# A graph-attention kernel: TensorE spreads the destinations' parts over the edge tiles in four parts, one in each group, instead of one burst per node tile

## The chip, the cores and the metric

The kernel runs on one core of one Trainium2 chip. The metric is device time in microseconds for one execution; 2591.09 us is the median of three runs (2585.95 to 2595.64) of the kernel before. The profile comes from a further execution, taken with the hardware profiler.

## The reference, cut to what matters

Two graph-attention (GAT) layers and a two-layer perceptron over 6250 nodes and 100000 edges that are sorted by destination, with a self-loop at each node:

```python
def gat_conv(x, src, dst, W, a_src, a_dst, bias, heads):
    h = (x @ W).reshape(n, heads, -1)
    alpha_s = (h * a_src[None]).sum(-1)
    alpha_d = (h * a_dst[None]).sum(-1)
    e = jax.nn.leaky_relu(alpha_s[src] + alpha_d[dst], NEG_SLOPE)
    m = jax.ops.segment_max(e, dst, num_segments=n)
    e = jnp.exp(e - m[dst])
    denom = jax.ops.segment_sum(e, dst, num_segments=n)
    alpha = e / (denom[dst] + 1e-16)
    out = jax.ops.segment_sum(h[src] * alpha[:, :, None], dst, num_segments=n)
    return out.reshape(n, -1) + bias
...
h = gat_conv(relu(layernorm(x)), src, dst, W1, a_src1, a_dst1, b1, 4)
h = gat_conv(relu(h), src, dst, W2, a_src2, a_dst2, b2, 1)
out = x + relu(relu(h) @ Wm1 + bm1) @ Wm2 + bm2
```

## The kernel before, in words

**Stages.** A first stage (until about 150 us of the profile) normalises x and multiplies it by W1, and stores one row for each node, features and source scores, in a table in device memory. Then `layer_edges` (L525) runs twice, for layer 1 with four heads and for layer 2 with one. While layer 1 runs over the edges it also makes layer 2's table (`Node1.steps`, L794); while layer 2 runs it also does the perceptron and writes the output (`Node2.steps`, L900). Between the two lies a short stretch (about 1430 to 1480 us) in which `prepare` (L464) and `first_whole` (L262) work.

**Tiling.** An edge tile holds 128 edges. Four edge tiles are a group `g`; four groups belong to a node tile `t` of 128 nodes, so `t, j = divmod(g, 4)` (L706). There are 49 node tiles and 196 groups in a layer. The order of the instructions is written out by hand: each engine executes its own instructions in the order of the program.

**One group.** `gather(g + AHEAD)` (L540, L709) has GpSimd issue four indirect DMAs, eight groups ahead, that fetch the rows of the edges' sources into `G`; ten such buffers exist. `pair(g, 0)` and `pair(g, 1)` (L611) treat two edge tiles each: ScalarE takes two exponentials of the source scores (L619, L621); VectorE multiplies by the destination's part `rho` (L624), takes the larger (L634 in layer 1, L627 in layer 2), and makes `hw` (L636 in layer 1: the weighted rows; L631 in layer 2: weighted one-hot matrices); TensorE sums over edges into `o_ps[g]` (L647), of which there are three buffers. `gather_up(g - 2)` (L658) comes at the end of a group: VectorE adds `o_ps` of the group two before to the running sum (`acc`, L672), ScalarE copies a quarter of it (`sum`, L680). `advance(g)` (L684) is called twice in a group and takes the node work of finished node tiles one step on: transposes (L761), `rT` (L767), `h_ps` (L812) and a table row in layer 1; `tp`/`m_ps` (L921), `mT` (L926) and `y_ps` (L937, L940) in layer 2.

**The destinations' parts.** An edge tile needs, for each of its edges, the destination's `rho`. `pre.win` holds `rho` of the nodes near each group, split into three bf16 parts. `mask[u]` is a one-hot matrix for two groups (eight edge tiles): in layer 1 VectorE makes it (`make_mask`, L559, L570) and the sync engine's queue (SP) stores it; in layer 2 SP loads it again (`fetch_mask`, L519). Six mask buffers exist. `meet(t)` (L591) multiplies the 16 mask tiles of node tile `t` with `win` into the PSUM tile `e_ps[t]`, of which there are two ("e"): 16 matmuls of 12 columns in layer 1 and of 3 columns in layer 2 (L599). `join(t)` (L602) has VectorE add the three parts for all 16 edge tiles in one instruction (L607); the sums are the `rho` that `pair` reads in the four groups of `t`.

**Order around the change.** At `j == 0` of node tile `t`, after `pair(g, 0)` and the first `advance`, `meet(t + 1)` issues all 16 matmuls (L724); `pair(g, 1)` follows. At `j == 3`, after `pair(g, 1)` and the second `advance`, comes `join(t + 1)` (L737), then `gather_up(g - 2)`. So the matmuls of `meet(t + 1)` stand three groups ahead of the VectorE instruction that reads their result.

Of the kernel before, what the change touches and what calls it, by code (L numbers as in the profile page):

```python
# [10 lines left out]
F32 = mybir.dt.float32  # L11
# [6 lines left out]
P = 128  # L18
# [11 lines left out]
TPG = 4  # L30
# [23 lines left out]
def kernel(  # L54
# [21 lines left out]
    nc = tc.nc  # L76
# [9 lines left out]
    ps = edges_stack.enter_context(tc.tile_pool(name="ps", bufs=2, space=bass.MemoryType.PSUM))  # L86
# [152 lines left out]
    def first_sources(layer):  # L239

        n = len(THERE[layer])
        sources[layer] = []
        for j in range(0, n, 8):
            m = min(n - j, 8)
            of = rowsp.tile([P, 16 * P], BF16, name="drow").bitcast(I32)
            nc.sync.dma_start(of[:, :m * P], bcast(src_rows, m * P, (FIRST + j) * P))
            sources[layer].append(of)
# [14 lines left out]
    def first_whole(pool, layer):  # L262

        j = 0
        for stage, (n, there) in enumerate(EARLY[layer]):
            if stage and layer == 1:
                first_hits(pool, layer, stage)
            for k in range(n):
                g, t = divmod(FIRST + j, TPG)
                G = first_G[layer][g][:, t]  # L270
                p = ps.tile([P, TW[layer]], F32, name="missing", tag="o", bufs=3)
                for T in range(there, NT):
                    nc.tensor.matmul(p, hits[stage, T][:, k * P:(k + 1) * P], kept[T][:, :TW[layer]],
                                     start=(T == there), stop=(T == NT - 1))
                nc.vector.scalar_tensor_tensor(G, G, first_ok[layer][:, j:j + 1], p, ALU.mult, ALU.add)
                j += 1
# [226 lines left out]
    drow, mask = {}, {}  # L503
# [9 lines left out]
    def fetch_rows(r):  # L513

        if r < NET // 16:
            drow[r] = rowsp.tile([P, 16 * P], BF16, name="drow")
            nc.sync.dma_start(drow[r], bcast(dmod_d, 16 * P, r * 16 * P))
# [7 lines left out]
    def layer_edges(layer, H, node, pre, matched, pre_pool):  # L525
# [4 lines left out]
        with tc.tile_pool(name=f"eg{layer}", bufs=4) as eg, \  # L530
# [3 lines left out]
            G, hot, e_ps, o_ps = {}, {}, {}, {}  # L534

            def tiles(g):

                return range(max(TPG * g, FIRST) - TPG * g, min(TPG * g + TPG, LAST) - TPG * g)

            def gather(g):  # L540
                if not 0 <= g < NG:
                    return
                if g in first_G[layer]:
                    G[g] = first_G[layer][g]
                else:
                    G[g] = gp.tile([P, TPG, max(TW.values())], F32, name="G")[:, :, :TW[layer]]
                for t in tiles(g):
                    k = TPG * g + t
                    if k < FIRST + len(THERE[layer]):
                        continue  # L550
                    nc.gpsimd.indirect_dma_start(  # L551
                        out=G[g][:, t], out_offset=None, in_=table[layer],
                        in_offset=bass.IndirectOffsetOnAxis(ap=src_i[:, k:k + 1], axis=0))


            def both(u):
                return tiles(2 * u)[0], TPG + tiles(2 * u + 1)[-1] + 1
# [16 lines left out]
            def make_hot(g):  # L574

                if layer == 2 or not 0 <= g < NG:
                    return
                T = tiles(g)
                k, n = TPG * g + T[0], len(T)
                hot[g] = eg.tile([P, TPG, P], F32, name="hot")  # L580
                nc.vector.tensor_tensor(  # L581
                    hot[g][:, T[0]:T[0] + n], iota_ps.unsqueeze(1).to_broadcast([P, n, P]),
                    dcol[:, k:k + n].unsqueeze(2).to_broadcast([P, n, P]), ALU.is_equal)

            def ranges(t):

                for u in (2 * t, 2 * t + 1):
                    a, b = both(u)
                    yield u, u % 2 * 8, a, b

            def meet(t):  # L591

                if t >= NT:
                    return
                e_ps[t] = ps.tile([P, 16, 6 * H], F32, name="e_ps", tag="e")
                for u, at, a, b in ranges(t):
                    m = mask.pop(u)
                    for k in range(a, b):
                        nc.tensor.matmul(e_ps[t][:, at + k, :3 * H], m[:, k * P:(k + 1) * P],  # L599
                                         pre.win[:, 2 * u + k // TPG + 1], start=True, stop=True)  # L600

            def join(t):  # L602
                if t >= NT:
                    return
                (_, _, a, _), (_, at, _, b) = ranges(t)
                T = slice(a, at + b)
                nc.vector.tensor_reduce(  # L607
                    e_ps[t][:, T, 3 * H:4 * H],
                    e_ps[t][:, T, :3 * H].rearrange("p t (h k) -> p t h k", k=3), AX.X, ALU.add)
# [40 lines left out]
            def stay_warm(n):  # L650

                if layer == 1:
                    for _ in range(n):
                        nc.tensor.matmul(idle_ps[0], idle[:, :P], idle, start=True, stop=True)
# [3 lines left out]
            def gather_up(g):  # L658

                if not 0 <= g < NG:  # L660
                    return
                last = g == NG - 1
                if last:

                    late.append(node.steps(NT - 1, None, run[0], o_ps.pop(g)))
                    return
                acc = sums.tile([P, RW[layer]], F32, name="acc")
                if g == 0:
                    nc.vector.tensor_copy(acc, o_ps.pop(g))
                else:  # L670
                    k = (g + 1) % 4
                    nc.vector.scalar_tensor_tensor(acc, run[0], keep[:, k:k + 1],  # L672
                                                   o_ps.pop(g), ALU.mult, ALU.add)
                run[0] = node.whole(NT - 1, acc) if g == NG - 2 else acc
                t, q = divmod(g - 2, 4)
                if 0 <= t < NT - 1:
                    if q == 0:
                        done[t] = sums.tile([P, RW[layer]], F32, name="sum", bufs=3)
                    r = slice(32 * q, 32 * q + 32)
                    nc.scalar.activation(done[t][r], acc[r], AF.Copy)  # L680
                    if q == 3:
                        late.append(node.steps(t, done.pop(t)))

            def advance(g):  # L684

                for _ in range(2 if NG - 4 <= g < NG - 2 else 1):
                    for step in list(late):
                        if next(step, 0) == 0:
                            late.remove(step)
# [10 lines left out]
            matched()  # L700
            if layer == 2:
                first_whole(pre_pool, layer)
            meet(0)
            join(0)
            for g in range(NG):
                t, j = divmod(g, 4)  # L706
                if g == NG - 2:
                    at_end.append(g)
                gather(g + AHEAD)  # L709
                pair(g, 0)  # L710
                if g == NG - 1:
                    pair(g, 1)
                if g >= NG - 2:
                    gather_up(g - 1)
                advance(g)
                if g <= NG - 4:
                    make_hot(g + 1)
                if g in (NG - 4, NG - 3):
                    make_hot(g + 2)
                if j == 0:  # L720
                    if layer == 1:
                        fetch_rows(t + 4)
                    node.prefetch(t)
                    meet(t + 1)  # L724
                elif j == (2 if t < NT - 1 else 1):
                    node.ahead(t)
                elif j % 2:
                    make_mask((g + 7) // 2)
                if g == NG - 3:
                    idle_ps.append(ps.tile([P, 4 * P], F32, name="idle_ps", tag="e"))  # L730
                if g >= NG - 3:
                    stay_warm(3)
                if g < NG - 1:
                    pair(g, 1)
                advance(g)
                if j == 3:
                    join(t + 1)  # L737
                if g < NG - 2:
                    gather_up(g - 2)
                if g == NG - 3:  # L740
                    gather_up(g - 1)
                if NG - 3 <= g < NG - 1:
                    stay_warm(3)
                G.pop(g)
                hot.pop(g, None)
                if layer == 1 and g == NG - 6:
                    first_sources(2)
# [505 lines left out]
```

## Time and profile before

| | us |
|---|---|
| median of three runs | 2591.09 |
| the profiled execution's own time | 2642.57 |
| its span in the profile | 2640.8 |
| layer 1 over the edges, about | 1230 (200 to 1430) |
| layer 2 over the edges, about | 1140 (1480 to 2620) |
| TensorE busy with matmuls, of the span | 1657.0 (63%) |
| GpSimd busy | 1598.5 (61%) |
| VectorE busy | 1415.1 (54%) |
| ScalarE busy | 560.3 (21%) |
| the 1564 matmuls of L599, busy | 55.7 |
| mean clock granted to TensorE | 0.764 of full speed |

The profile covers one execution from the first instruction to the last. "Busy" counts the time in which at least one instruction of the group was at work; matmuls overlap, so 1564 of them at 167 ns each are busy for 55.7 us only. An instruction's "idle before" is the time that its engine stood still ahead of it, and the arrow names what ended that: an instruction that had just finished; "issue", where nothing shown had just released it; or "remote", where a semaphore had just moved and the profile finds no instruction that ended then. In this kernel, on one core, "remote" is no other core.

### The profile page before, as it was taken

The numbers are of one execution on the slowest core, as the hardware profiler recorded it, in microseconds if no ns is written. First come the engines' busy times: TensorE is split into PE (matmuls) and PEld (weight loads), VectorE is DVE, ScalarE is ACT, GpSimd is POOL, SyncE is SP. The second block draws the span as 40 slices with busy tenths as digits, with TensorE's granted clock in tenths as the row PEclk, the third lists the DMA queues.
The fourth block names the chain that finished last, engine by engine and source line by source line (L and its number), as shares of the span: only waits on it lengthen the run. The fifth ranks groups of instructions, "written<-read, shape, count | busy, mean of one in ns | idle before, by whom it ended". The sixth has DMA issues, their size and how long they took to land. (4 is left out here: it accounts for less than half of the span.)

```text
span 2640.8 us, 26321 instructions
## 1 busy us (share of the span) xinstructions
PE 1657.0 (63%) x6763; PEld 1115.4 (42%) x6765; DVE 1415.1 (54%) x4359; ACT 560.3 (21%) x2601; POOL 1598.5 (61%) x1759
## 2 busy tenths in 40 slices
PE   9955556554655555555457366766666676676676
PEld 7843333333433333333335244444444444444454
DVE  7935556555655555555556354444445444444454
ACT  5521111111111111111112122222222222222122
POOL 7865666655665556556653666666666666666661
PEclk9977766777677677777778677787787778787878
DMA  9944445444444444444443444454444444454442
GB/s 358 339 144 145 136 126 145 124 136 122 134 138 127 133 130 138 129 129 136 130 117 105 132 128 130 146 151 146 139 140 150 146 138 142 146 151 144 131 150 75
DMA packets 157541, 383.24 MB, mean 145 GB/s; under 512 B 35543, under 2 KB 49966, under 8 KB 157382
## 3 DMA queue, kind: packets, MB, share of 16 engines
q0 software_dynamic: 75072, 209.10, 29.2%
q1 hardware_dynamic: 80940, 170.88, 19.2%
q10 hardware_dynamic: 1370, 1.48, 0.2%
q8 instruction: 58, 0.95, 0.1%
q14 instruction: 101, 0.83, 0.1%
HBM read 323.13 MB, written 58.19 MB: 144 GB/s over the span
## 5 line engine op out<-in xcount | busy, mean ns | idle before, releaser
L551 POOL DMA_INDIRECT G<-table,src_i x1545 | 1467.8, 950 | 908.1 <-issue 747.6
L647 PE MATMUL o_ps<-hw,hot 128*128 128x260 f32 x1564 | 604.3, 520 | 532.7 <-DVE hw L636 216.3
L647 PEld LDWEIGHTS o_ps<-hw,hot 128*128 128x128 f32 x1564 | 353.9, 248 | 750.2 <-DVE hw L636 301.4
L647 PE MATMUL o_ps<-G,hw 128*128 128x258 f32 x1564 | 500.2, 455 | 208.3 <-issue 107.6
L647 PEld LDWEIGHTS o_ps<-G,hw 128*128 128x128 f32 x1564 | 337.0, 227 | 342.8 <-issue 156.7
L680 ACT ACTIVATE sum<-acc 32x260 f32<-32x260 f32 (+1 forms) x384 | 159.9, 416 | 1489.1 <-DVE acc L672 829.4
L624 DVE TENSOR_TENSOR e_ps<-e,e_ps 128x8 f32<-128x8 f32 (+1 forms) x782 | 127.7, 163 | 561.5 <-ACT e L621 359.5
L672 DVE SCALAR_TENSOR_TENSOR acc<-acc,keep,o_ps 128x260 f32<-128x260 f32 (+1 forms) x388 | 185.3, 478 | 220.4 <-remote 203.7
L631 DVE TENSOR_SCALAR hw<-iota_ps,dcol,w 128x128 f32<-128x128 f32 x782 | 285.0, 406 | 31.4 <-DVE w L627 17.5
L636 DVE TENSOR_TENSOR hw<-G,e_ps 128x520 f32<-128x520 f32 x391 | 271.9, 695 | 48.3 <-DVE e_ps L634 29.8
L937 PE MATMUL y_ps<-wm,mT 128*128 128x384 f32 x392 | 197.2, 621 | 105.0 <-issue 60.6
L619 ACT ACTIVATE e<-G 128x8 f32<-128x8 f32 (+1 forms) x782 | 155.4, 199 | 95.0 <-issue 30.2
L937 PEld LDWEIGHTS y_ps<-wm,mT 128*128 128x128 f32 x392 | 82.4, 231 | 182.1 <-issue 119.8
L621 ACT ACTIVATE e<-G 128x8 f32<-128x8 f32 (+1 forms) x782 | 150.2, 192 | 0.0
L940 DVE TENSOR_TENSOR y<-y_ps,xt 128x384 f32<-128x384 f32 (+1 forms) x98 | 54.2, 553 | 175.5 <-remote 127.7
L346 PE MATMUL h_ps<-w,r 128*128 128x256 f32 x588 | 133.0, 380 | 4.3 <-ACT r L337 4.3
L581 DVE TENSOR_TENSOR hot<-iota_ps,dcol 128x512 f32<-128x512 f32 (+1 forms) x196 | 133.6, 682 | 0.0
L346 PEld LDWEIGHTS h_ps<-w,r 128*128 128x128 f32 x588 | 108.0, 190 | 21.7 <-ACT r L337 5.5
L767 ACT ACTIVATE rT<-tp,bT 128x128 f32<-128x128 f32 x196 | 60.2, 357 | 217.7 <-remote 175.8
L634 DVE TENSOR_TENSOR e_ps<-e_ps,e 128x8 f32<-128x8 f32 x391 | 68.1, 174 | 54.9 <-remote 29.8
L921 PE MATMUL tp<-rT,wm 128*128 128x128 f32 x392 | 64.9, 318 | 29.0 <-ACT rT L767 27.8
L921 PEld LDWEIGHTS tp<-rT,wm 128*128 128x128 f32 x392 | 61.9, 230 | 40.3 <-ACT rT L767 35.3
(405 smaller groups left out, 1175.0 us busy)
## 6 DMA issues: line engine op xcount, KB each, us to landing
xt<-in_x SPq DMA_DIRECT2D x96, 384.0 KB
drow<-dmod_d SPq DMA_DIRECT2D x49, 512.0 KB
mask_d<-mask SPq DMA_DIRECT2D x98, 256.0 KB
mask<-mask_d SPq DMA_DIRECT2D x98, 256.0 KB
G<-table,src_i POOLq DMA_INDIRECT x1545
xTt<-in_xT SPq DMA_DIRECT2D x49, 384.0 KB
out<-y SPq DMA_DIRECT2D x48, 384.0 KB
table<-kept SPq DMA_DIRECT2D x49, 132.0 KB
```

The source lines that it names most:

```text
L346: nc.tensor.matmul(h_ps, r[:, k], w1[:, k], start=(k == 0), stop=(k == KI - 1))
L551: nc.gpsimd.indirect_dma_start(out=G[g][:, t], out_offset=None, in_=table[layer], in_offset=bass.IndirectOffsetOnAxis(ap=src_i[:, k:k + 1] ...
L581: nc.vector.tensor_tensor(hot[g][:, T[0]:T[0] + n], iota_ps.unsqueeze(1).to_broadcast([P, n, P]), dcol[:, k:k + n].unsqueeze(2).to_broadca ...
L619: nc.scalar.activation(e1, sc, AF.Exp)
L621: nc.scalar.activation(e2, sc, AF.Exp, scale=SLOPE)
L624: nc.vector.tensor_mul(v, e2, rho)
L631: nc.vector.tensor_scalar(hw[:, t], iota_ps, dcol[:, k:k + 1], w[:, t], ALU.is_equal, ALU.mult)
L636: nc.vector.tensor_mul(hw, Gp[:, :, :RW[1]].rearrange("p t (h c) -> p t h c", h=H), w.unsqueeze(3).to_broadcast([P, 2, H, C + 1]))
L647: nc.tensor.matmul(o_ps[g], l, r[:, :RW[layer]], start=(k == tiles(g)[0]), stop=(k == TPG - 1))
L672: nc.vector.scalar_tensor_tensor(acc, run[0], keep[:, k:k + 1], o_ps.pop(g), ALU.mult, ALU.add)
L680: nc.scalar.activation(done[t][r], acc[r], AF.Copy)
L937: nc.tensor.matmul(y_ps, mT[:, j], wm2[:, j, s * half:(s + 1) * half], start=False, stop=(j == KH - 1))
```

## The change

`meet` takes a list of groups. Ahead of the loop it is called for all four groups of node tile 0; in the loop it is called in every group, for the group's own quarter of the next node tile, between the group's middle work and `pair(g, 1)`. It makes the PSUM tile at its first part, and gives up a mask buffer after the second of the two groups that use it. `join` stays where it was.

```diff
-            def meet(t):
+            def meet(t, js):
                 if t >= NT:
                     return
-                e_ps[t] = ps.tile([P, 16, 6 * H], F32, name="e_ps", tag="e")
-                for u, at, a, b in ranges(t):
-                    m = mask.pop(u)
-                    for k in range(a, b):
-                        nc.tensor.matmul(e_ps[t][:, at + k, :3 * H], m[:, k * P:(k + 1) * P],
-                                         pre.win[:, 2 * u + k // TPG + 1], start=True, stop=True)
+                if t not in e_ps:
+                    e_ps[t] = ps.tile([P, 16, 6 * H], F32, name="e_ps", tag="e")
+                for j in js:
+                    g = 4 * t + j
+                    for k in tiles(g):
+                        at = (j % 2 * TPG + k) * P
+                        nc.tensor.matmul(e_ps[t][:, TPG * j + k, :3 * H], mask[g // 2][:, at:at + P],
+                                         pre.win[:, g + 1], start=True, stop=True)
+                    if j % 2:
+                        mask.pop(g // 2)
...
-            meet(0)
+            meet(0, range(4))
             join(0)
             for g in range(NG):
                 t, j = divmod(g, 4)
...
                     node.prefetch(t)
-                    meet(t + 1)
...
                 if g >= NG - 3:
                     stay_warm(3)
+                meet(t + 1, (j,))
                 if g < NG - 1:
                     pair(g, 1)
                 advance(g)
                 if j == 3:
                     join(t + 1)
```

The number of matmuls, their operands and their results are the same.

## The prediction

> **What bounds the kernel now.** I read the page first, then the stages one by one, then who waits for whom, and then the instructions of single groups. The page shows no engine that is busy throughout:
>
> ```profile
> PE 1657.0 (63%) x6763; PEld 1115.4 (42%) x6765; DVE 1415.1 (54%) x4359; ACT 560.3 (21%) x2601; POOL 1598.5 (61%) x1759
> L551 POOL DMA_INDIRECT G<-table,src_i x1545 | 1467.8, 950 | 908.1 <-issue 747.6
> ```
>
> GpSimd's gathers need at least 0.95 + 0.30 = 1.25 us each where they run without a pause, so 5.0 us for a group of four. A group takes 1230 / 196 = 6.3 us in layer 1 and 1140 / 196 = 5.8 us in layer 2. The gathers are therefore close, but they don't set the pace; they pause for buffers. The list of waits says on what the others stand still:
>
> ```profile
> DVE acc L672 <- remote: 203.7, 25, 11.3
> DVE y L940 <- remote: 127.7, 22, 11.4
> ACT rT L767 <- remote: 175.8, 28, 11.7
> ACT mT L926 <- remote: 90.1, 11, 14.6
> ```
>
> (us in total, times, longest.) All four read what TensorE wrote. Together 597 us in 86 waits: the largest loss in the 2370 us of the two edge stages. One of them, in layer 1:
>
> ```profile
> 603.19 0.44 PE L761 MATMUL tp<-ident,o 128*128 128x128 f32 x2
> 603.47 0.55 PE L599 MATMUL e_ps<-win,mask 128*128 128x12 bf16 x16
> 604.81 1.15 PE L647 MATMUL o_ps<-hw,hot 128*128 128x260 f32 x4 [0.79 <-issue]
> ...
> 612.54 0.69 DVE L636 TENSOR_TENSOR hw<-G,e_ps 128x520 f32<-128x520 f32 x1
> 613.29 1.14 PE L647 MATMUL o_ps<-hw,hot 128*128 128x260 f32 x4
> ...
> 624.38 0.48 DVE L672 SCALAR_TENSOR_TENSOR acc<-acc,keep,o_ps 128x260 f32<-128x260 f32 x1 [11.15 <-remote]
> ```
>
> The burst of `meet` at 603.47 marks group j = 0. The `acc` at 624.38 is that group's sum, taken at the end of j = 2; its last matmuls are those of 604.81, done at 605.96. VectorE got the news 18.4 us later. In between TensorE started more matmuls, and VectorE worked on for two groups, because `acc` asks only for the group two before; then it stood for 11 us. I call this a withheld result. Why TensorE withholds it, the trace doesn't show. So the time of a stretch is the groups' own pace, about 4.3 us (4.2 us between the `acc` at 604.67 and that at 608.87, some are longer), plus what is left of each withheld result after VectorE's lead over TensorE is used up. **That lead, about two groups, is what the change touches.**
>
> [...] after 612.54 nothing runs on VectorE until 624.38. [...] The 86 waits fall on some 11,800 TensorE instructions of the edge stages (matmuls and weight loads in the table by stage), one in 137[...]. The change keeps the number of matmuls, so I take the number of withheld results as unchanged.
>
> **The change, part by part.** Sums are made against the profiled execution: 2640.8 us of span, 2642.57 us of its own time; the median of the runs is 2591.09, 2% less, and I scale by that.
>
> *The burst at j = 0 goes.* 16 matmuls take 0.55 us, and TensorE idles 0.79 us right behind them: nothing waits for that time. 96 bursts at 0.55 us are 53 us of TensorE work, and the same 53 us come back in quarters of about 0.14 us. I take zero for the saving. Bounds: nothing, or half the 53 us (26 us) if in layer 2, where TensorE is often in arrears, `pair(g, 1)` starts earlier for it and VectorE feels it.
>
> *Waits of the parts.* Part 0 stands where the burst stood and takes over its waits on the PSUM buffer. The mask for parts 2 and 3 is now wanted two groups later: no loss. Masks are freed one and three groups later; they are written again eight groups after their last use in layer 1, and the loads on SP's queue in layer 2 may start at most three groups later than now, some six groups ahead of their place. What follows them on SP, x loads and output stores, has that cover too. Cost zero; if the cover failed, a few us at the first tiles only.
>
> *`join` waits for a fresh result.* This is the one added wait. Now `join` reads matmuls three groups old and waits once in the whole kernel:
>
> ```profile
> L607 DVE TENSOR_REDUCE e_ps<-e_ps x98: 206/272/360, 202.9 to 2604.1; 128x64 f32<-128x192 f32 x48, 128x16 f32<-128x48 f32 x48, 128x56 f32<-128x168 f32 x1, 128x14 f32<-128x42 f32 x1
>   remote: 24.2, 1
> ```
>
> After the change part 3 stands on TensorE behind the four matmuls of `pair(g, 0)` of the same group, j = 3. In layer 1 VectorE still does `hot` (0.68), a mask (0.50) and `pair(g, 1)` (1.1) after that pair, which covers it mostly. In layer 2 it has only `pair(g, 1)`:
>
> ```profile
> 2077.61 0.73 DVE L631 TENSOR_SCALAR hw<-iota_ps,dcol,w 128x128 f32<-128x128 f32 x2
> 2077.83 2.78 PE L647 MATMUL o_ps<-G,hw 128*128 128x258 f32 x12
> 2078.65 0.73 DVE L631 TENSOR_SCALAR hw<-iota_ps,dcol,w 128x128 f32<-128x128 f32 x2
> 2079.29 0.21 DVE L607 TENSOR_REDUCE e_ps<-e_ps 128x16 f32<-128x48 f32 x1
> 2079.40 0.48 DVE L672 SCALAR_TENSOR_TENSOR acc<-acc,keep,o_ps 128x258 f32<-128x258 f32 x1
> ```
>
> I took, for each of 48 node tiles in each layer, the end of that pair's fourth matmul, added 0.18 us for the part (four of 0.034 us, and its end), and compared it with the start of `join`. In layer 1 `join` would wait in 18 of 48, 6.9 us in all; in layer 2 in 48 of 48, 34.5 us in all, 0.7 us each. Behind it queue `acc`, then ScalarE's `sum` and the exponentials, then the next `pair`: the loop that sets the pace. But in layer 2 TensorE itself is behind at that point (12 matmuls in a row above) and has work while VectorE waits. I take 5 of the 6.9 and 15 of the 34.5: **20 us**; bounds 0 and 41.
>
> *Withheld results meet `join`.* If the withholding starts in j = 2 or early in j = 3, VectorE now stops at `join` at the end of j = 3; before it could go on to the next `acc`, up to two groups. I placed the long idle times of VectorE in the node tile. Layer 1: all at the end of j = 2 (16), the end of j = 3 (8) or within j = 2 (the rest), so none lies past `join` and would move. Layer 2: at j = 2, j = 0 right behind `join` (10 waits for `mT`, 76 us) and j = 1 (16 waits at L940, 111 us). Those at j = 0 move by one `acc`, hidden. Of those at j = 1 most begin with the `y_ps` matmuls, which stand behind part 3; about four begin earlier and would lose a group, 4 us. That gives **16 us**. Bounds: where the withholding begins depends on the order of TensorE's instructions, which changes. Spread evenly, 0.25 of a node tile loses 1 group and 0.1 loses 2, so 0.45 groups x 4.3 us x 86 = 166 us on top; and a better place could give back about 0.1 group, 0.4 us, at each of the 86, so I allow 40 us.
>
> **Sum.** 0 + 20 + 16 = 36 us: a span of 2677 us, times 2591.09 / 2640.8, gives 2626 us, 1.4% slower.
>
> **The rivals.**
> - *No difference*: VectorE's waits at `join` fall in time that TensorE needs anyway, as layer 2's arrears suggest, and withheld results sit where they do now. For it: VectorE stands idle for 588 of layer 2's 1140 us already. 2593 us.
> - *Much slower*: withheld results start in j = 2 and 3 and `join` takes the lead away: half of the bound, 80 us, and the 36: 2705 us. For it: 0.35 of the tile is exposed. Against it: layer 1 shows none there now.
> - *Faster*: burst gone, TensorE takes up `pair(g, 1)` of j = 0 at once, and withheld results that now cling to the burst (24 of layer 1's waits are for j = 0's or j = 1's sums) shift to where the lead hides more. Price 26 to 40 us, less 5 for `join`: 2565 us. It decides if layer 2's `join` costs under 10 us.
> - *The change doesn't do what it says*: a part that must wait for the join's tile as a whole would show at L599; I see no reason and give it nothing.
>
> **Numbers.** A measurement of this kernel tells about 0.5% (13 us) from no change. Forecast 0.45, no difference 0.22, much slower 0.18, faster 0.15. The forecast's own range is 2600 to 2660. Range for 8 in 10: 2568 to 2695, which cuts into both outer cases. Faster by over 0.5%: 0.14; within: 0.25; slower: 0.61.
>
> **What would show it.** Right: L607 has idle time before it in layer 2, some 0.3 to 0.7 us each and L599 comes in fours. The withheld part: "remote" waits at L607 of several us. Wrong: L607 waits under 10 us in all, or the sum of the "remote" waits at L672, L940, L767 and L926 falls well below 597 us.

## The result, and the profile after

| | before | after |
|---|---|---|
| median of the runs on the same chip, us | 2588.52 (4 runs) | 2747.29 (4 runs) |
| ratio, with its 95% interval | | 1.0617 [1.0578, 1.0657] |
| the profiled execution's own time, us | 2642.57 | 2745.21 |
| one node tile in layer 1, from `join` to `join`, mean, us | 25.40 | 27.92 |
| one node tile in layer 2, mean, us | 23.84 | 23.44 |

The change made the kernel 159 us slower; 36 us had been forecast. The profiled execution of before ran 54 us over its median, so the two profiles differ by 103 us only: 47 node tiles of layer 1 at 2.52 us more each are 118 us, and 47 of layer 2 at 0.40 us less are 19 us. So the 103 us lie in layer 1. Before's profile being long, e4 and e3 below are the better pair: before and after with the same small alteration, on one chip, each profile within 0.1% of its median. There a node tile takes 25.30 and 28.32 us in layer 1, 23.88 and 23.76 in layer 2, which says the same.

Lines move by 5 in the changed kernel: `join` is L612, the part's matmuls L602, `acc` L677, `rT` L772, `y` L945, `o_ps` L652. The page of after (engines; then the groups of lines, with the idle time ahead of each and what ended it):

```profile
PE 1606.0 (59%) x6764; PEld 1107.4 (40%) x6765; DVE 1422.7 (52%) x4359; ACT 558.1 (20%) x2601; POOL 1596.4 (58%) x1759
...
L551 POOL DMA_INDIRECT G<-table,src_i x1545 | 1465.5, 949 | 1028.1 <-issue 877.2
...
L612 DVE TENSOR_REDUCE e_ps<-e_ps 128x64 f32<-128x192 f32 (+2 forms) x98 | 28.5, 291 | 563.0 <-remote 502.2
```

Every engine does the same work in the same busy time as before, only spread over more time. VectorE stood 563 us ahead of `join`, where it had stood 24. The list of waits of after says what became of the four waits shown of before:

```profile
DVE e_ps L612 <- remote: 502.2, 50, 15.7
...
DVE y L945 <- remote: 170.7, 27, 11.0
...
ACT rT L772 <- remote: 65.3, 15, 7.2
...
ACT mT L931 <- remote: 11.5, 2, 9.7
...
DVE acc L677 <- remote: 8.6, 2, 7.8
```

The waits at `acc` fell from 203.7 us to 8.6, those at `rT` and `mT` from 265.9 to 76.8; `join` took 502.2. The five together are 758 us, where the four of before were 597. One node tile of layer 1 in the timeline of after (start, duration, engine, line, operation; in brackets the idle time before it):

```profile
600.58 0.25 PE L602 MATMUL e_ps<-win,mask 128*128 128x12 bf16 x4
...
601.02 0.69 DVE L641 TENSOR_TENSOR hw<-G,e_ps 128x520 f32<-128x520 f32 x1
...
601.77 1.97 PE L652 MATMUL o_ps<-hw,hot 128*128 128x260 f32 x4 [0.94 <-DVE hw L641]
...
612.10 0.37 DVE L612 TENSOR_REDUCE e_ps<-e_ps 128x64 f32<-128x192 f32 x1 [10.39 <-remote]
...
614.83 1.67 PE L652 MATMUL o_ps<-hw,hot 128*128 128x260 f32 x3 [11.09 <-DVE kept L821]
```

The last part (four matmuls at 600.58) was done at 600.83 (the profile models the ends of matmuls, but TensorE began its next four at 601.77), and `hw` of the same group kept VectorE busy until 601.71. The part's result was there for TensorE, but VectorE got the news at 612.10, 11.3 us after its end. TensorE itself had run out of work at 603.74 and got none until VectorE went on. So both stood, and nothing of VectorE's work passed the waiting `join`: in both profiles `acc` is VectorE's next instruction behind each of the 96 `join`s of the loops. Before the change `join` read matmuls three groups old, and VectorE would have passed it.

In layer 2 the fresh part looks as forecast (again after, where nothing was withheld):

```profile
1680.38 2.09 PE L652 MATMUL o_ps<-G,hw 128*128 128x258 f32 x4 [2.08 <-DVE hw L636]
...
1682.26 0.29 PE L602 MATMUL e_ps<-win,mask 128*128 128x3 bf16 x4
1682.41 1.88 PE L652 MATMUL o_ps<-G,hw 128*128 128x258 f32 x4
1682.59 0.22 DVE L612 TENSOR_REDUCE e_ps<-e_ps 128x16 f32<-128x48 f32 x1 [0.91 <-issue]
```

The part stands behind the four matmuls of the same group, and `join` waits 0.91 us for it.

### The profile page after: what moved, and what is told of

It reads as the page before. It is cut to its first block, busy times and chain, and to the rows that moved or that the text cites. A ratio compares the mean times of both kernels' runs of the same rounds, so it can differ in the third digit from the quotient of the medians.

```text
span 2743.4 us, 26322 instructions
## 1 busy us (share of the span) xinstructions
PE 1606.0 (59%) x6764; PEld 1107.4 (40%) x6765; DVE 1422.7 (52%) x4359; ACT 558.1 (20%) x2601; POOL 1596.4 (58%) x1759
## 4 chain that ended last, share of the span: by engine, by line
DVE 30%; another core or an unknown queue 25%; issue 18%; PE 17%; ACT 6%; DMA 3%; POOL 0%; SPq 0%; ACTq 0%; POOLq 0%; DVEq 0%
DVE hw L641 7%; PE o_ps L652 7%; DVE hw L636 5%; PE h_ps L346 4%; PE y_ps L942 3%; ACT sum L685 3%; DVE e_ps L629 3%; DVE acc L677 3%; DMA drow<-dmod_d 2%; DVE e_ps L639 2%; DVE mask L570 2%; DVE w L632 2%; ACT e L624 1%; DVE hot L581 1%
## 5 line engine op out<-in xcount | busy, mean ns | idle before, releaser
L652 PE MATMUL o_ps<-hw,hot 128*128 128x260 f32 x1564 | 574.6, 502 | 703.9 <-DVE kept L821 482.1
L652 PEld LDWEIGHTS o_ps<-hw,hot 128*128 128x128 f32 x1564 | 335.2, 237 | 857.2 <-DVE kept L821 505.0
L652 PE MATMUL o_ps<-G,hw 128*128 128x258 f32 x1564 | 507.9, 460 | 205.7 <-DVE hw L636 113.6
L652 PEld LDWEIGHTS o_ps<-G,hw 128*128 128x128 f32 x1564 | 321.2, 224 | 307.6 <-DVE hw L636 146.4
L612 DVE TENSOR_REDUCE e_ps<-e_ps 128x64 f32<-128x192 f32 (+2 forms) x98 | 28.5, 291 | 563.0 <-remote 502.2
L942 PE MATMUL y_ps<-wm,mT 128*128 128x384 f32 x392 | 190.5, 618 | 8.0 <-ACT mT L931 7.6
L677 DVE SCALAR_TENSOR_TENSOR acc<-acc,keep,o_ps 128x260 f32<-128x260 f32 (+1 forms) x388 | 184.5, 476 | 20.4 <-issue 11.6
L945 DVE TENSOR_TENSOR y<-y_ps,xt 128x384 f32<-128x384 f32 (+1 forms) x98 | 54.1, 552 | 200.1 <-remote 170.7
L602 PEld LDWEIGHTS <-mask 128*128 128x128 bf16 x1564 | 108.1, 106 | 99.6 <-issue 42.1
L602 PE MATMUL e_ps<-win,mask 128*128 128x12 bf16 (+1 forms) x1564 | 101.5, 171 | 24.6 <-DVE mask L570 15.9
L878 PE MATMUL y_ps<-bm2r,ones_r 3*128 3x384 bf16 x98 | 36.5, 374 | 131.3 <-issue 117.6
```

The costliest lines, as they stand in the source:

```text
L602: nc.tensor.matmul(e_ps[t][:, TPG * j + k, :3 * H], mask[g // 2][:, at:at + P], pre.win[:, g + 1], start=True, stop=True)
L652: nc.tensor.matmul(o_ps[g], l, r[:, :RW[layer]], start=(k == tiles(g)[0]), stop=(k == TPG - 1))
L942: nc.tensor.matmul(y_ps, mT[:, j], wm2[:, j, s * half:(s + 1) * half], start=False, stop=(j == KH - 1))
```

## The experiments

All ratios are against the kernel before on the same chip. The chips differ, and no number can be understood without this: in three series of runs, on two chips or three, the kernel before took 2588.52, 2632.35 and 2586.69 us, and the traces have the withheld results; in four, on four other chips, it took 2142.08, 2137.82, 2135.23 and 2140.15 us, and they have none. I call them chips **with** and **without**. Which one a run got was chance. No chip is known to have been of both kinds; whether it is the chip or its condition at the time, the runs don't show.

**Theory: freshness.** On chips with, TensorE's results are withheld about once in a node tile, whatever the change does; what counts is how many groups of work VectorE has between the issue of the matmuls that it waits for and the wait. **Rivals:** the spreading itself costs (four short interruptions in place of one); the end of GpSimd's run of gathers, which depends on VectorE, is what brings the news; the change costs by itself, without withheld results; the count of TensorE's instructions sets where the withholding falls.

### How many groups of lead: e1_three, e2_late_burst, and the burst at j = 1

The parts are placed otherwise, against the kernel after:

```diff
-                meet(t + 1, (j,))
+                meet(t + 1, {0: (0,), 1: (1,), 2: (2, 3), 3: ()}[j])
```

> Parts at j = 0, 1 and 2 (two parts at j = 2), none at j = 3. If the loss is that join reads a result that is too fresh, the last part is now a group older and layer 1's 10.4 us waits at join go: 2590 to 2620 us. If the spreading itself costs (TensorE's stream cut into parts), it stays near the changed kernel: 2720 to 2750 us.

```diff
-                meet(t + 1, (j,))
+                if j == 3:
+                    meet(t + 1, range(4))
```

> All 16 matmuls in one burst at j = 3, no spreading. Fresh result: as slow as the changed kernel, 2730 to 2780 us, with 10 us waits at join in layer 1. Spreading: as fast as before, 2580 to 2610 us.

And one burst at j = 1 (`if j == 1: meet(t + 1, range(4))`), which fell on a chip without in its first two runs (e8_burst_j1, e10_burst_j1_again) and on one with in the third (f2_burst_j1):

> All 16 matmuls in one burst at j = 1. By the lead theory join's lead is then two groups, that of acc itself, so it costs little: 0 to 1.5% over before. If any later place costs in proportion to its distance from j = 0: about 2% over before.

> The kernel after with all 16 matmuls issued in group j = 1, two groups ahead of join, once more. Theory A, lead counts in groups: where remote waits exist, a ratio of 0.995 to 1.015, as two groups are the lead that acc has anyway; join waits remote under 150 us. Theory C (any place but j = 0 costs, since the burst at j = 0 itself gives TensorE its pause at a good place): 1.03 or more. Where no remote waits exist: 0.998 to 1.002 for both.

> All 16 matmuls of meet issued in group j = 1, two groups ahead of join, for a chip on which the kernel before has remote waits. Theory A (lead counts in groups, and acc has two groups anyway): ratio 0.995 to 1.015 and remote waits at join under 150 us. Theory C (any place later than j = 0 exposes join in proportion, as 1.0245 with one group and 1.059 with none): 1.01 to 1.03. On a chip without: 1.000 within 0.002.

On the chips without, the burst at j = 1 took 0.9999 [0.9990, 1.0008] (e8) and 1.0001 [0.9992, 1.0009] (e10) of the time before, which says nothing on the lead. Measured on chips with. "Long waits" are all idle times of VectorE over 3.5 us, wherever they stand, in layer 1 from the first `join` of its loop to the last, 47 node tiles:

| last part issued | groups ahead of `join` | ratio | long waits in layer 1: count, mean us, sum us | node tile in layer 1, us |
|---|---|---|---|---|
| j = 0 (before) | 3 | 1 | 30, 7.9, 238 | 25.40 |
| j = 1, one burst (f2) | 2 | 1.0083 [1.0050, 1.0115] | 45, 5.0, 225 | 25.15 |
| j = 2, three parts (e1) | 1 | 1.0245 [1.0211, 1.0279] | 44, 8.8, 388 | 26.75 |
| j = 3, four parts (after) | 0 | 1.0617 [1.0578, 1.0657] | 44, 10.3, 452 | 27.92 |
| j = 3, one burst (e2) | 0 | 1.0590 [1.0562, 1.0617] | 44, 10.5, 463 | 28.19 |

The row of `join` in the lists of waits, of e1_three, then e2_late_burst, then f2_burst_j1:

```profile
DVE e_ps L612 <- remote: 425.5, 51, 18.5
```

```profile
DVE e_ps L612 <- remote: 615.4, 62, 15.7
```

```profile
DVE e_ps L612 <- remote: 76.8, 10, 10.7
```

One burst at j = 3 costs as much as four parts that end there: the intervals overlap, and the waits are alike (10.3 and 10.5 us). So it isn't the spreading. Each group of lead takes something off. With two groups, which `acc` has anyway, 10 remote waits remain at `join`, and the kernel loses 0.8%; with three, one. The long waits with a later `join` come 44 or 45 times in 47 node tiles, with the lead of before only 30 times. That a withheld result then also comes in the others, and VectorE's lead covers it, is argued from these counts; no view shows it. Before's profiled execution was 2% over its median, so its layer 1 can't be set against f2's to the tenth; e4 below, with the old place of the burst and on the chip of e1 and e2, has 28 such waits of 8.2 us and 25.30 us for the node tile, which agrees with it.

### Does GpSimd's run of gathers end the withholding? e3_after_ahead7, e4_before_ahead7

```diff
-AHEAD = 8
+AHEAD = 7
```

in the kernel after (e3) and in the kernel before (e4).

> The changed kernel with gathers seven groups ahead and nine buffers instead of ten. If TensorE's late news comes only when GpSimd's run of gathers has ended for want of buffers, the run ends one group (5 us) earlier and layer 1's waits at join fall from 10.4 to about 5.4 us: 48 x 5 = 240 us less, 2500 to 2560 us. If the delay has its own length, they stay at 10 us and the time at 2740 us or above.

> The kernel before with gathers seven groups ahead and nine buffers. If the end of the run of gathers ends the late news: its 86 waits shorten by up to 5 us each, 2300 to 2500 us. If the delay has its own length: 2590 us or some per cent more, as gathers start later.

In layer 1 of after, GpSimd's gathers go on for 7.5 us of a long wait and stop, for want of a free buffer, 2.9 us before its end (medians). The waits at `join` in layer 1 stayed as they were, 10.4 us on average in e3 and 10.3 in after, and e3 took 1.0549 [1.0523, 1.0575]. But the alteration didn't move what it was to move: in e3 the gathers also stop 7.5 us into the wait and 3.1 us before its end. `gather(g + AHEAD)` takes over the buffer of group g - 2, with ten buffers as with nine. So this pair doesn't test the idea. The traces at hand do show that the end of a run isn't always needed: in layer 2 of after, 14 of the 44 remote waits of VectorE and ScalarE over 3.5 us end in the middle of a run (the `y` at 2020.78 us after 7.01 us, with gathers started at 2019.92 and 2021.17), and 10 of 34 in layer 1 of before. In layer 1 of after none of 43 does. Whether the stop plays a part there stays open. e4 took 0.9976 [0.9962, 0.9990], a gain of 0.2%; it is smaller than the 0.5% that was set as the bound.

### Does the change cost anything without withheld results? e9_after_again

The changed kernel, unaltered.

> The changed kernel as it is, on whichever chip this run gets. Theory A (the whole loss is withheld results of TensorE that now meet join): where the kernel before takes about 2590 to 2630 us, the ratio is 1.055 to 1.067 with 450 to 560 us of remote waits at join; where it takes about 2142 us and its trace has no remote waits, nothing is left to meet join, the gathers at 1.25 us set the pace, and the ratio is 0.995 to 1.005, with join waiting under 1 us in each node tile. Theory B (join's wait for a matmul just issued costs by itself, as it delays the buffers of the gathers): on the chip without remote waits still 1.01 to 1.05.

It fell on a chip without: 2137.41 against 2137.82 us, a ratio of **1.0000 [0.9992, 1.0009]**. The top of its list of waits, and what the answer for `join`'s line says on its idle time:

```profile
DVE e_ps L629 <- ACT e L626: 596.5, 495, 5.0
ACT e L624 <- DMA G<-table,src_i: 569.4, 410, 5.2
POOL G L551 <- issue: 362.2, 1185, 1.5
```

```profile
L612 DVE TENSOR_REDUCE e_ps<-e_ps x98: 200/270/359, 176.3 to 2094.8; 128x64 f32<-128x192 f32 x48, 128x16 f32<-128x48 f32 x48, 128x56 f32<-128x168 f32 x1, 128x14 f32<-128x42 f32 x1
its engine sat idle before it (us, times) until:
who waited for it (us, times):
```

Nothing stands under "sat idle": the freshest part never held `join` up. ScalarE waits for gathers, VectorE for ScalarE, and GpSimd pauses only for the 0.3 us between one gather and the next (362 us in 1185 times). A node tile takes 19.7 us in layer 1 and 19.9 in layer 2; 16 gathers at 1.25 us are 20.0. The gathers set the pace, and what the change adds lies beside it. So the change by itself costs nothing here, and the rival that it does fell.

### Are the gathers behind the withheld results? Plain loads

Each gather is replaced by a plain load of a fixed block of 128 rows; what is summed over the edges is then other than the reference's.

```diff
-                    nc.gpsimd.indirect_dma_start(
-                        out=G[g][:, t], out_offset=None, in_=table[layer],
-                        in_offset=bass.IndirectOffsetOnAxis(ap=src_i[:, k:k + 1], axis=0))
+                    r = k % 40 * P
+                    nc.sync.dma_start(G[g][:, t], table[layer][r:r + P])
```

> The kernel before, in which each edge tile gets a fixed block of 128 table rows by a plain load on SP's queue in place of the rows of its sources by GpSimd's indirect DMA (the 19 of the first tiles apart), so it computes something else. If GpSimd's gathers are what makes TensorE announce results late, the remote waits of 597 us nearly vanish and the time falls to 1900 to 2150 us. If TensorE does it whatever GpSimd does (its own instruction stream), the remote waits stay above 400 us and the time above 2350 us.

> The changed kernel with the same plain loads. Gathers are the cause: join's 10.4 us waits in layer 1 shrink to under 1 us and the kernel is within 1% of the other one with plain loads. TensorE's own stream: join still waits about 10 us in each node tile of layer 1, and it stays 5 to 7% behind the other.

> The kernel before with each indirect gather replaced by a plain load of a fixed block of 128 rows, on SP's queue; what it computes over the edges is therefore other than the reference's. Theory D (GpSimd's gathers[...] make TensorE's results late): no remote waits, and a time near 1822 us on any chip. Theory E (the withholding is TensorE's or the chip's own): on a chip where the kernel before has some 600 us of remote waits, 200 us of them or more stay, and the time is over 1900 us.

> The kernel before with each indirect gather replaced by a plain load of a fixed block of 128 rows on SP's queue (what it computes over the edges is other than the reference's), for a chip on which the kernel before has remote waits. Theory D (GpSimd's gathers make TensorE's results late): no remote waits at acc, rT, y and mT, and 1820 to 1900 us. Theory E (the withholding is TensorE's or the chip's own): 200 us of them or more stay, and the time is over 1950 us. On a chip without remote waits: 1820 us again, which tells nothing.

On chips without, 1822.45 us (e5, before) and 1825.27 (e6, after), and 1821.51 again (e11). There was nothing to take away, so they told nothing of the cause. f1 fell on a chip with, where the kernel before takes 2586.69 us, and took **1822.38 us**, 0.705 [0.7015, 0.7085]. The engines in f1, and the only remote wait of VectorE in its list:

```profile
PE 1444.8 (79%) x6764; PEld 987.0 (54%) x6765; DVE 1401.2 (77%) x4359; ACT 553.0 (30%) x2601; POOL 130.9 (7%) x214
```

```profile
DVE G L275 <- remote: 1.4, 1, 1.4
```

Without gathers the withheld results are gone, and the two kinds of chip take the same time within 0.1%. So the gathers bring the withheld results, on the chips with. What of them does it, their issue on GpSimd, their scattered rows or their packets, this run doesn't separate.

### Does the number of TensorE instructions set it? The matmuls twice

Each matmul of `meet` in the kernel before is issued twice, with the same result.

```diff
-                    for k in range(a, b):
+                    for k in [k for k in range(a, b) for _ in range(2)]:
```

> The kernel before with each of meet's matmuls issued twice: 32 more TensorE instructions in a node tile, 30% more in layer 1, still in the burst at j = 0 and with 0.55 us more work there. If late news comes once in some number of TensorE instructions[...], there are 20 to 30% more remote waits, 120 to 180 us: 2700 to 2780 us. If it hangs on something else (time, gathers), the waits stay as they are and the time rises by under 1%.

> The kernel before with each matmul of meet issued twice, once more: 1564 more matmuls, and as many weight loads, with the same results. Theory F (withheld results come once in so many TensorE instructions[...]): where remote waits exist, 25% more of them, 86 to about 107, and 60 to 120 us more time. Theory G (their number follows from other things, such as the node tile or the gathers): 86 within 10, and under 30 us more. Where none exist: within 0.3% of before for both.

> The kernel before with each matmul of meet issued twice, for a chip on which the kernel before has remote waits. Theory F (withheld results come once in so many TensorE instructions): about 107 remote waits in place of 86 and 60 to 120 us more. Theory G (they come with the node tile or the gathers): 76 to 96 and under 30 us more. On a chip without: 1.000 within 0.003.

On chips without, 1.0006 [0.9997, 1.0015] and 1.0005 [0.9996, 1.0014]: nothing. On the chip with, f3 took 1.0587 [1.0539, 1.0634], 152 us more, and both theories of its expectation missed. In its list of waits:

```profile
DVE acc L672 <- remote: 301.6, 35, 10.5
PEld L599 <- issue: 267.1, 205, 3.4
```

The remote waits at `acc`, `join`, `y`, `rT` and `mT` are 79, not 107. Other waits hide some: VectorE's long waits in both layers are 94, where before had 78, so the count alone doesn't decide. The spacing speaks against once in so many instructions. Layer 1's long waits lie 140 TensorE instructions apart in f3 (median) and 108 in after; both are one node tile, with 16 gathers. What grew is their length and the number that shows: 42 long waits of 9.3 us in layer 1, 389 us, where before had 30 of 7.9. Here `join` reads old matmuls, as before, and the wait stands at `acc`. So **freshness at `join` is not the only way to lose this time**: more instructions of TensorE at j = 0 did it too. TensorE also stopped 205 times, 1.3 us each, at its own burst (before: 7 times). Why, I can't say. The traces do show that such stops have a step. Three of them in layer 2 of before, 2.13 us from start to start:

```profile
2284.41 0.80 PE L937 MATMUL y_ps<-wm,mT 128*128 128x384 f32 x1 [2.04 <-issue]
2286.54 0.80 PE L937 MATMUL y_ps<-wm,mT 128*128 128x384 f32 x1 [1.33 <-issue]
2288.67 0.80 PE L937 MATMUL y_ps<-wm,mT 128*128 128x384 f32 x1 [1.33 <-issue]
```

Take the matmuls of the edge stages that follow a stop of over 0.3 us ended by "issue", where the matmul ahead had one of over 0.3 us too. In f3 all 262, and in before 112 of 120, start 0.7 us or a small multiple of it (mostly 1.4, 2.1 or 2.8) after the one ahead, within 0.06 us. No trace of a chip without has such a matmul, nor has f1. Of the 120 in before, 89 start while VectorE stands in a wait of over 3.5 us, though such waits fill only 598 us. So in a withheld stretch it isn't only TensorE's news that comes late: where TensorE has work, it goes on in slow steps itself. VectorE isn't free of it either: in the edge stages of before it stood 84 times for over 0.3 us, 81 us in all, until its own last instruction released it; in e9 3 times, 1 us.

### Is it once in 16 gathers or once in a node tile? Half the gathers

In both kernels every second gather of a group became a plain load, as above (`if t % 2:` ahead of it).

> The kernel before with every second gather of a group replaced by a plain load of a fixed block of 128 rows on SP's queue (what it computes over the edges is other than the reference's), for a chip on which the kernel before has remote waits. Theory H (withheld results come once in 16 gathers, wherever these stand): long idle times of VectorE (over 3.5 us) are two node tiles apart, about 36 to 45 in place of 73 in the edge stages, and the time is near 1820 us plus half of what withheld results cost, 1950 to 2150 us. Theory I (they come once in a node tile, as long as there are gathers): 70 or more, and over 2200 us. Theory J (GpSimd must be issuing without a pause for it): under 10, and under 1900 us. On a chip without remote waits: 1820 to 1850 us.

> The kernel after with the same half of the gathers replaced (what it computes over the edges is other than the reference's). Theory H: remote waits at join about half of 502 us, 200 to 300, and 40 to 100 us over the run before it. Theory I: 400 us or more, and 100 to 170 us over it. Theory J: under 30 us, and within 10 us of it.

> The kernel before with every second gather of a group replaced by a plain load of a fixed block (what it computes over the edges is other than the reference's), once more. Theory H (withheld results come once in 16 gathers): on a chip with remote waits 36 to 45 long idle times of VectorE (over 3.5 us) in the edge stages in place of 73, and 1950 to 2150 us. Theory I (once in a node tile while there are gathers): 70 or more, and over 2200 us. Theory J (GpSimd must be issuing without a pause): under 10, and under 1900 us. On a chip without: 1820 to 1850 us again, and the question stays open.

All three fell on chips without: 1822.42 (before), 1823.05 (after), 1819.85 us (before). They can't tell the two apart, and the question stays open. They do show that on such chips half the gathers are hidden completely: the times are those of plain loads throughout (e5 1822.45, e11 1821.51).

## Why the prediction was wrong

- **What bounds the kernel: right in kind.** Withheld results were named as the largest loss, and VectorE's lead over TensorE as what the change touches. Both held. The prediction also said that gathers don't set the pace. That is so on this chip (GpSimd stood 908 us ahead of them before and 1028 after), but f1 shows that they bring the waits that do.
- **The burst at j = 0 goes, waits of parts and masks: zero, right.** With no withheld results all of it together is 1.0000 [0.9992, 1.0009], under 2 us either way.
- **`join` waits for a fresh result: right in size, and free.** 34.5 us of such waits were expected in layer 2; without the 11 long ones (74 us) `join` waited 32 us there, typically 0.9 us. 15 us were charged to the time, but layer 2's node tile did not grow (23.84 to 23.44 us; e4 to e3, 23.88 to 23.76). That VectorE would have waited there for other things anyway, as the rival "no difference" had it, fits this and is not shown singly.
- **Withheld results meet `join`: this step failed.** It counted 16 us, on the ground that in layer 1 "none lies past `join` and would move". After the change 42 long waits, 433 us, stand at `join` in layer 1, nearly one in each node tile. From the first `join` to the last VectorE's idle time in layer 1 rose from 518 to 632 us, 113 us, and the layer by 118. The working took the places where VectorE *stood* before the change for the places where results were *withheld*, and took these as fixed. Where VectorE stands is where its lead runs out. With the lead gone it stands at the next fresh result, and the period then settles on the node tile: in after it is 28.65 us, with 16 gathers, in 40 long waits of layer 1 nearly without exception; in before the median was 30 us, and a quarter were 63 or more. The same step took the number as unchanged: the long waits of both layers went from 78 to 94.
- **The bound was there and was not used.** Spread evenly, 0.45 of a group at each of 86 waits gave 166 us on top. The loss is 159. The rival "much slower" had the right mechanism at half that bound, 2705 us, with a chance of 0.18, and the range ended at 2695. Its only counter-argument was the placing that failed.
- **A stall by the count of TensorE's instructions: not borne out.** The prediction counted one wait to 137 of them. A stall by count would keep its count of instructions between long waits; it went from 108 in after to 140 in f3, where the matmuls were doubled, and the waits vanished with the gathers in f1 (one remote wait of VectorE, 1.4 us), whose instructions are not TensorE's. Nor do the packets of the queue that the pages list as `q8 instruction`, 16 KB each, come as often as the waits: there are 58 in before and after, and 70 in f3, 12 more for 3128 more instructions of TensorE, one in about 260. In layer 1 of after 20 of them fall between the first `join` and the last, where 42 long waits stand at `join`.
- **The signs named beforehand were too weak.** L612 waits in layer 2, L602 comes in fours, remote waits stand at `join`: all came true, for a loss four times the forecast. The sum of the waits at the four old places would have been the better sign: it fell from 597 to 256 us, which the prediction had listed as a mark of being wrong, and the difference, and more, was at `join`.

What stays open: why gathers make TensorE's results late on some chips and not on others, what the period counts, what the step of 0.7 us is, and how more matmuls at j = 0 expose the waits as well. No version here that computes the same beats both kernels by more than 0.2%.

## What to carry to other kernels

A wait that never shows in the profile may be covered by the distance between an instruction and the one that reads it; before you shorten that distance, ask what the longest delay is that the trace shows anywhere for this kind of result (here 10 to 18 us), and price the change as if that delay fell there every time, unless something fixes its place. Where an engine stands tells where its lead ran out, not where the delay began. And run the kernel before on more than one chip: here the same edit costs 6.2% on one and 0.0% on another, and the larger prize by far is in the gathers (0.705 of the time with plain loads, which compute something else).

## What the runs showed of the hardware

- Chips of one kind ran the kernel before in 2588, 2632 and 2587 us, others in 2135 to 2142 us, 17 to 19% less. With plain loads both take 1822 us (f1 1822.38, e5 1822.45).
- On the first kind the trace has 12,870 changes of semaphores (before) or 14,702 (after), on the second 42,669 for the same kernel as after (e9). Until the gathers begin, at about 143 us, the counts agree (3194 in after, 3211 in e9); then most are missing on the first kind. That so many waits are called "remote" there fits this. Why they are missing, no run shows. f1, on a chip of the first kind, has 42,266 changes in 1819.6 us, where the same kernel on the second kind (e5) has 42,663 in 1821.4: so their rate alone isn't it, and gathers bring the missing records and the withheld results together. Which of the two brings the other, or whether one thing brings both, no run here shows.
- On the first kind, in withheld stretches, TensorE starts its matmuls in steps of about 0.7 us (262 of 262 in f3, 112 of 120 in before); on the second kind no trace has such stops (in e9 one matmul follows a stop of over 0.3 us ended by "issue": 2.6 us at L273, in `first_whole`, outside the loops over the edges).
- On the second kind 16 gathers at 1.25 us (20.0 us) bound a node tile of 19.7 to 19.9 us (e9), and with half of them as plain loads the bound is gone (f4: 1822.42 us, the kernel before on that chip 2135.23).
